# The weights' places cut into pieces, and the products of the projections' weights made in the head

## The chip, the core and the metric

The kernel runs on one NeuronCore of one Trainium2 chip. The metric is the time of one execution on the device in microseconds (us). The engines are named as in the profile: PE is TensorE (its matmuls; PEld its weight loads), DVE is VectorE, ACT is ScalarE, POOL is GpSimd, and SP is SyncE, which issues most of the transfers. All data are fp32.

## The reference

x holds 4 images of 128 channels and 64 x 64 pixels, so S = 4096 positions. Two layers follow one another, and the parts that the change touches are in the second one:

```
# layer 0
v = group_norm(x)
e1, e2 = prelu(w1 v), prelu(w2 v)                       # 64 channels each
asm = prelu(wa v)
x = x + softmax(e1^T e2, over the keys) applied to asm
# layer 1, tokens t = the positions of x, of 128 channels
n = layer_norm(t)
t = t + softmax((n Wq^T)(n Wk^T)^T / 128) (n Wv^T)
n = layer_norm(t)
p = softmax over the S tokens of (n gate + gate_b)      # 64 experts
vals, idx = top 8 tokens of each expert
pooled = sum over the 8 of vals * n[idx]                # one row for each expert and image
h = gelu([pooled, 1] weight1)                           # 128 -> 512, each expert its own
o = [h, 1] weight2                                      # 512 -> 128
t[idx] += vals * o
```

An expert's weight1 is 128 x 512 and its weight2 512 x 128, 256 KB each. All 64 experts are read once, 32 MiB, for only 4 rows each.

## The kernel before, in words

The kernel is one program with a fixed order on every engine. It goes through eight attention stages, `stage(b, layer, ...)`, in the order (image, layer) = (0,0), (1,0), (0,1), (2,0), (1,1), (3,0), (2,1), (3,1). A stage has 8 blocks n of 512 queries, and each block has 8 groups g of 512 keys. In a group PE makes the scores `ps` (L560), ACT their exponentials `pt` (L569), and PE the sums `av` (L494 for layer 0, L522 for layer 1, where DVE and PE also use combinations of tiles, `tt`, to save products). Work of other stages is given to a stage as a Python generator (`beside`, `ahead`); the stage takes one step of it in each group, so that PE makes it between two groups.

Ahead of the first stage lies the head. SP and ACT issue the 8 pieces of the first image, `first_x`; ACT then issues all the constants (`const_load`); `group_norm(0)` makes the statistics with DVE (`gn_st`), PE (`gn_pm`, `gn_pv`) and POOL (`gn_y`), and the first two blocks' convolutions (`pe`, `pa`, with their PReLU in `ye`, `te`, `ya`, `ta`) give the first operands.

`weights_qk()` makes the products of the projections' weights once: the transposes `pwq`, `pwk` (each copied to SBUF), their product `wqk`, and `wvd` with its sums `wtwo`, `wsum`. Before the change it is the last part of the generator beside the stage (0,0). The last row of weight1, a bias, is loaded as `w1b` and transposed by four PE transposes `pw` in stage (3,1), in `first_weights()`.

After the last stage comes the route of image 3 (`last_route`, `last_scores`), and then the expert products, in 16 groups g of 4 experts (EG). For each group `first_product` makes `ph` (copied to `hp`), `hidden` makes the transposes `pht`, adds the bias and applies the gelu (`hT`), and `second_product` makes `po`. A group's weights are 2 MiB, packed in DRAM by earlier transfers (`wp`), in two halves of 1 MiB: half 0 for `ph`, half 1 for `po`. They are loaded by SP into *places* in SBUF. A place before the change is one tile of 16 KB in each partition. There are nine:

- places 0 and 1 are the keys and values of the last stage, which come free late in it,
- 6, 7 and 2 are tiles of the pools `seq` and `extra`, loaded in stage (3,1),
- 3, 4 and 5 are a pool `ring`, opened when the pool `att` is closed after the last stage,
- 8 is `late_place`, in a pool `late`, opened when the pool `blk` is closed after the route.

A half is reloaded with group g + 9 when group g's product with it is made. A DMA on SP goes out in program order, and one that waits holds what stands behind it.

The softmax weights of image 3 are made on DVE, ACT and POOL in `last_scores`: a MATCH_REPLACE (L806) and two DVE steps that are spread between the groups, then exponentials on ACT (L985) and differences on POOL (L987). At the end, `first_pair` (the weights of images 0 and 1, 2 MiB) and `x2_pair` (the residual, 4 x 2 MiB) are loaded into places; PE makes `px` (L1276), DVE adds it to the residual (L1283), and ACT issues the stores (L1286).

`watch` and `keep_busy` are small extra instructions of PE and DVE that the kernel puts between parts of the program. They compute nothing that is returned.

Of the kernel before, what the change touches and what calls it, by code (L numbers as in the profile page):

```python
# [15 lines left out]
P = 128  # L16
BLK = 512
# [9 lines left out]
def tile_unshifted(  # L27
# [91 lines left out]

    def const_load(name, shape, src):  # L120
        t = const.tile(shape, F32, tag=name, name=name)
        nc.scalar.dma_start(out=t, in_=src)
        return t


# [9 lines left out]
    aa = const_load("aa_sb", [P, 1], a["aa"].partition_broadcast(P))  # L135
    wqT = const_load("wqT_sb", [P, P], a["WqT"])
    wkT = const_load("wkT_sb", [P, P], a["WkT"])
    wv = const_load("wv_sb", [P, P], a["WvT"])
    gate = const_load("gate", [P, E], a["gateT"])
    gate_b = const.tile([P, 1], F32, tag="gate_b", name="gate_b")  # L140
    w2b = const.tile([P, O], F32, tag="w2b", name="w2b")
    for h in range(2):
        half = slice(h * E, (h + 1) * E)
        nc.scalar.dma_start(out=gate_b[half, :], in_=a["gate_b"])
        nc.scalar.dma_start(out=w2b[half, :], in_=a["weight2"][:, H, :])

# [286 lines left out]
    def weights_qk():  # L433
        wT = []
        for nm, w in (("q", wqT), ("k", wkT)):
            pw = ms_tile(f"pw{nm}")
            nc.tensor.matmul(pw[:, :P], lhsT=w, rhs=unfold, start=True, stop=True)
            t = block_tile("te", f"w{nm}")[:, :P]
            nc.vector.tensor_copy(t, pw[:, :P])
            wT.append(t)  # L440
        yield
        pw = ms_tile("pwqk")
        nc.tensor.matmul(pw[:, :P], lhsT=wT[0], rhs=wT[1], start=True, stop=True)
        nc.vector.tensor_copy(wqk, pw[:, :P])
        yield
        pw = ms_tile("pwv")
        nc.tensor.matmul(pw[:, :P], lhsT=unfold, rhs=wv, start=True, stop=True)
        nc.vector.tensor_copy(wvd[:, :C], pw[:, :P])
        nc.vector.tensor_copy(wvd[:, C : C + 1], last[:, 0:1])
        lo, hi = slice(0, HC), slice(HC, C)  # L450
        for half in (lo, hi):
            nc.scalar.copy(wtwo[half, :], wvd[hi, :])
            nc.scalar.copy(wsum[half, :], wvd[lo, :])
        nc.vector.tensor_add(wsum, wsum, wtwo)
        yield
# [177 lines left out]
    def finish_attn(b, n):  # L633
# [28 lines left out]
        xq = resid.pop((b, 1, n)).rearrange("p (s c) -> p s c", c=C)  # L662
        xT = block_tile("inv", f"xT{nm}").rearrange("p (s c) -> p s c", c=C)
        for k, (s0, ns) in enumerate(((2, 2), (0, 2)) if final else ((0, 3), (3, 1))):
# [309 lines left out]
    def last_scores(b, top, neg):  # L974

        hs = half_of(b)
        m = M[b // 2][hs, :]
        z = late_place[hs, :]

        tc.keep_in_program_order(replace(b, top, z))  # L980
        yield
        for part in QUARTERS:
            for t in (z, m):
                tc.keep_in_program_order(
                    nc.scalar.activation(t[:, part], t[:, part], AF.Exp, bias=neg[hs, :])  # L985
                )
            nc.gpsimd.tensor_sub(m[:, part], m[:, part], z[:, part])  # L987
        yield
# [81 lines left out]

    packing = iter(())
    run(group_norm(0, first_x))
    first_conv = conv(0, first_x)
    for _ in range(2):
        next(first_conv)
    run(query(0, 0, 0))
    tc.no_sync_barrier()


    W, places_of = {}, {}  # L1080

    def place(i, t):
        if len(t.shape) == 3:
            t = t.rearrange("p j c -> p (j c)")
        places_of[i] = t.rearrange("p (h x) -> p h x", h=2)

    def new_place(i, pool, tag):
        place(i, pool.tile([P, 2 * EG * H], F32, tag=tag, name=f"w{i}"))

    def load(g, i, h):  # L1090
        W[g] = places_of[i]
        nc.sync.dma_start(out=W[g][:, h, :], in_=packed[g][:, h, :])

    w1bT = const.tile([P, NHC, E], F32, tag="w1bT", name="w1bT")

    def first_weights():

        watch(0)
        w1b = block_tile("xq", "w1b", 4)[:E, :]
        nc.sync.dma_start(out=w1b, in_=a["weight1"][:, D1 - 1, :])  # L1100
        yield from idle(2)
        new_place(6, seq, "k")
        new_place(2, extra, "w")
        for g in (6, 2):
            for h in range(2):
                load(g, g, h)
        yield from idle(2)
        pw = ms_tile("pw")
        for c in range(NHC):
            nc.tensor.transpose(  # L1110
                pw[:, bass.ts(c, E)], w1b.rearrange("e (p c) -> e c p", c=NHC)[:, c, :],
                ident[:E, :E],
            )
        nc.scalar.copy(w1bT.rearrange("p c e -> p (c e)"), pw[:, : NHC * E])
        yield from idle(2)
        new_place(7, seq, "v")
        for h in range(2):
            load(7, 7, h)
        yield

    def last_weights(n, g):

        if (n, g) == (0, 0):
            place(0, keys[B - 1, 1])
            place(1, values[B - 1, 1])
        if n == NB - 1:
            if g == NG // 2 - 1:
                load(0, 0, 0)
            if g == NG // 2:
                load(1, 1, 0)  # L1130
            if g == NG - 1:
                load(0, 0, 1)

    stage(0, 0, chain(group_norm(1), conv(1), weights_qk()), (1, 0), ahead=first_conv, pace=(4, 3))
    packing = pack_weights()
# [13 lines left out]

    ends["att"].close()  # L1150
    pooledT = seq.tile([P, E, PAD], F32, tag="mixed", name="pooledT", bufs=1)
    nc.gpsimd.memset(pooledT, 0.0)
    nc.gpsimd.tensor_copy(pooledT[:, :, 0 : B - 1], pooled[:, :, 0 : B - 1])
    while after:
        step_after()
    ring = ctx.enter_context(tc.tile_pool(name="ring", bufs=3, reuse_waits="tile"))
    load(1, 1, 1)
    for g in range(3, 6):
        new_place(g, ring, "w")
        for h in range(2):  # L1160
            load(g, g, h)
    keep_busy(FILL[4], "busy_d")
    last_top = last_route(B - 1, pooledT)
    ends["blk"].close()
    late = ctx.enter_context(tc.tile_pool(name="late", bufs=1, side="right", reuse_waits="tile"))
    late_place = late.tile([P, S], F32, tag="z", name="late_place")
    place(8, late_place)
    scores = last_scores(B - 1, *last_top)
    watch(1)

    for h in range(2):
        load(8, 8, h)
    outT = late.tile([P, B, E], F32, tag="outT", name="outT")
    osb = late.tile([P, E // EG, O], F32, tag="osb", name="osb")
    half_g = E // EG // 2
# [3 lines left out]
    def first_product(g):  # L1179
        ph = ms_tile(f"ph{g}")  # L1180
        for j in range(EG):
            nc.tensor.matmul(  # L1182
                ph[bass.ts(j, PAD), :], lhsT=pooledT[:, g * EG + j, :],
                rhs=W[g][:, 0, bass.ts(j, H)], start=True, stop=True,
            )
        hps[g] = hp = late.tile([P, H], F32, tag="hp", name=f"hp{g}", bufs=2)
        nc.vector.tensor_copy(hp, ph)

    def hidden(g):
        pt, hp = pht[:, g % 2, :], hps.pop(g)  # L1190
        for c in range(NHC):
            nc.tensor.transpose(  # L1192
                pt[:, bass.ts(c, P)], hp.rearrange("p (q c) -> p c q", c=NHC)[:, c, :], ident
            )
        hTs[g] = hT = late.tile([P, NHC, EG, PAD], F32, tag="hT", name=f"hT{g}", bufs=2)
        nc.vector.tensor_tensor(
# [5 lines left out]
    def second_product(g):  # L1202
        half, k = divmod(g, half_g)
        if k == 0:
            pos[half] = sc_tile(f"po{half}").rearrange("p k c -> p (k c)").rearrange(
                "p (g o) -> p g o", o=O
            )
        w2 = W[g][:, 1, :].rearrange("p (e c o) -> p e c o", e=EG, c=NHC)
        hT = hTs.pop(g)
        for c in range(NHC):  # L1210
            for j in range(EG):
                nc.tensor.matmul(  # L1212
                    pos[half][bass.ts(j, PAD), k, :], lhsT=hT[:, c, j, :], rhs=w2[:, j, c, :],
                    start=(c == 0), stop=(c == NHC - 1),
                )
        if k == half_g - 1:
            nc.vector.tensor_copy(osb[:, bass.ts(half, half_g), :], pos[half])
            for q in range(half * half_g // EG, (half + 1) * half_g // EG):
                by_expert(q)

    def by_expert(q):

        pt = ms_tile(f"pot{q}")
        for k in range(EG):
            nc.tensor.transpose(pt[:, bass.ts(k, P)], osb[:, q * EG + k, :], ident)
        nc.vector.tensor_copy(
# [4 lines left out]
    for g in range(E // EG + 2):  # L1231
# [6 lines left out]

        for half, now in ((0, g), (1, g - 2)):
            if 0 <= now and now + 9 < E // EG:  # L1240
                load(now + 9, now, half)
        if g == half_g + 2:
# [4 lines left out]

    M[0] = places_of[7].rearrange("p h x -> p (h x)")
    tc.keep_in_program_order(nc.sync.dma_start(out=M[0], in_=first_pair))
    WIDE = 2 * BLK  # L1250
    HS = S // 2
    ys = []
    for i in range(B // 2):
        for q in range(2):
            ys.append(places_of[2 * i + q])
            tc.keep_in_program_order(
# [7 lines left out]
    for i in range(B // 2):  # L1264
# [7 lines left out]
        for n in range(NB):  # L1272
            px = sc_tile(f"px{i}_{n}")
            for h in range(2):
                hs = slice(h * E, (h + 1) * E)
                nc.tensor.matmul(  # L1276
                    px[:, h, :], lhsT=oe[hs, :], rhs=M[i][hs, bass.ts(n, BLK)],
                    start=True, stop=True,
# [552 lines left out]
```

## Time and profile before

| | us |
|---|---|
| median of 3 runs (lowest to highest) | 3269.55 (3269.16 to 3271.02) |
| the profiled execution | 3268.95 |
| its span | 3267.2 |
| busy: PE | 3227.5 (99% of the span) |
| busy: DVE | 2123.3 (65%) |
| busy: ACT | 1255.6 (38%) |
| busy: POOL | 425.4 (13%) |
| DMA, mean over the span | 68 GB/s |
| DMA, last of 40 equal slices | 398 GB/s |

The span runs from the first instruction to the last one of the profiled execution; its time also holds what lies around them. Busy shares are means over the whole span. The head and the end are short against it, so the means say nothing of them: they are read from the chain of waits (what released each piece of work, followed back from the end), the timeline, and tables by stretches of time.

### The profile page before, as it was taken

Reading aid. Unit: us, or ns where it says so; the run is one execution under the profiler, and the core shown is the slowest. Engines: PE = TensorE matmul, PEld = TensorE weight load, DVE = VectorE, ACT = ScalarE, POOL = GpSimd, SP = SyncE. Lnnn points to the kernel's source line nnn. Section 1 sums busy time; section 2 is a strip of 40 time slices with the busy share of each in tenths; the row PEclk is TensorE's granted clock in tenths of the full one; section 3 lists DMA queues with packets and bytes.
Section 4 is the critical chain, followed back from the end, with each engine's and each line's share of the span. In section 5 each row is a group of like instructions: output and inputs, shape, how many; then the busy total and the mean of one; then the engine's idle time right before and its main releaser. Section 6 shows DMA issues by size and latency. Waiting matters only on the chain.

```text
span 3267.2 us, 49620 instructions
## 1 busy us (share of the span) xinstructions
PE 3227.5 (99%) x19856; PEld 1544.2 (47%) x19856; DVE 2123.3 (65%) x4191; ACT 1255.6 (38%) x1437; POOL 425.4 (13%) x414
## 2 busy tenths in 40 slices
PE   8999999999999999999999999999999999999997
PEld 4444444444554544444554444444445444445453
DVE  6665567556676667755675657775676566676566
ACT  3333434333333345333333335333333333343332
POOL 0111112310000004141000002242100002010011
PEclk9999999999999999999999999999999999999998
DMA  3121244223333222311221111321131111131149
GB/s 84 52 55 27 58 112 120 76 78 89 84 80 86 58 53 53 68 36 30 49 43 30 38 29 39 88 68 26 40 71 37 33 28 32 23 105 43 27 184 398
DMA packets 364242, 222.93 MB, mean 68 GB/s; under 512 B 273504, under 2 KB 298336, under 8 KB 358624
## 3 DMA queue, kind: packets, MB, share of 16 engines
q1 hardware_dynamic: 358544, 208.15, 23.8%
q10 hardware_dynamic: 4944, 10.46, 0.8%
q8 instruction: 158, 2.59, 0.3%
q0 software_dynamic: 512, 1.05, 0.1%
q14 instruction: 84, 0.69, 0.1%
HBM read 159.75 MB, written 97.19 MB: 79 GB/s over the span
## 4 chain that ended last, share of the span: by engine, by line
PE 97%; DVE 1%; DMA 1%; issue 0%; POOL 0%; ACT 0%; SPq 0%; ACTq 0%; DVEq 0%; POOLq 0%
PE ps L560 41%; PE av L494 27%; PE av L522 24%; PE pe L273 1%; PE pq L463 1%; PE pv L681 1%; PE pa L301 1%; DMA tt<-x 1%; PE pg L748 0%; PE ph L1182 0%; PE pd L608 0%; PE po L1212 0%; PE pht L1192 0%; PE px L1276 0%; DMA first_x<-in_x_dram 0%
## 5 line engine op out<-in xcount | busy, mean ns | idle before, releaser
L569 ACT ACTIVATE pt<-ps 128x1024 f32<-128x1024 f32 x1024 | 1022.2, 1025 | 1514.6 <-PE ps L560 1432.3
L560 PE MATMUL ps<-q,t 128*64 128x512 f32 x4096 | 924.8, 592 | 0.0
L494 PE MATMUL av<-pt,asm 64*128 64x512 f32 x4096 | 922.7, 589 | 0.9 <-ACT sw L652 0.9
L584 DVE TENSOR_TENSOR sacc<-sacc,pt 128x1024 f32<-128x1024 f32 x448 | 586.4, 1309 | 288.1 <-ACT pt L569 262.7
L522 PE MATMUL av<-pt,tt 128*64 128x256 f32 x3072 | 636.2, 379 | 0.0
L494 PEld LDWEIGHTS av<-pt,asm 64*128 64x128 f32 x4096 | 397.0, 187 | 484.5 <-issue 468.4
L508 DVE TENSOR_TENSOR tt<-pt 128x512 f32<-128x512 f32 x512 | 354.2, 692 | 356.3 <-ACT pt L569 339.8
L522 PE MATMUL av<-tt,mixed 128*64 128x256 f32 x2048 | 525.6, 379 | 0.0
L560 PEld LDWEIGHTS ps<-q,t 128*64 128x64 f32 x4096 | 292.2, 137 | 489.2 <-issue 458.1
L522 PEld LDWEIGHTS av<-pt,tt 128*64 128x64 f32 x3072 | 353.9, 137 | 290.8 <-issue 143.4
L560 PE MATMUL ps<-e,e 64*128 64x512 f32 x2048 | 490.0, 596 | 0.5 <-ACT ye L275 0.5
L522 PE MATMUL av<-tt,tt 128*64 128x256 f32 x1024 | 304.7, 379 | 0.0
L522 PE MATMUL av<-pt,mixed 128*64 128x256 f32 x1024 | 304.6, 379 | 0.0
L560 PEld LDWEIGHTS ps<-e,e 64*128 64x128 f32 x2048 | 192.6, 187 | 228.1 <-issue 223.1
L522 PEld LDWEIGHTS av<-tt,mixed 128*64 128x64 f32 x2048 | 280.5, 137 | 2.7 <-DVE tt L508 0.2
L182 POOL TENSOR_TENSOR l_y<-l_v,mhalf 128x4 f32<-128x4 f32 x64 | 64.8, 1013 | 1612.6 <-DVE l_v L181 1612.3
L510 DVE TENSOR_TENSOR tt<-pt 128x256 f32<-128x256 f32 x512 | 220.4, 431 | 16.4
L509 DVE TENSOR_TENSOR pt<-tt,pt 128x256 f32<-128x256 f32 x512 | 219.7, 429 | 16.2
L522 PEld LDWEIGHTS av<-pt,mixed 128*64 128x64 f32 x1024 | 140.2, 137 | 72.9 <-DVE pt L509 0.3
L522 PEld LDWEIGHTS av<-tt,tt 128*64 128x64 f32 x1024 | 140.1, 137 | 1.5 <-DVE tt L510 0.3
L603 POOL TENSOR_TENSOR all_sum<-all_sum,c 128x512 f32<-128x512 f32 x32 | 44.0, 1376 | 515.4 <-DVE c L602 515.4
L183 DVE TENSOR_TENSOR l_z<-l_y 128x4 f32<-128x4 f32 x64 | 13.9, 217 | 91.5 <-POOL l_y L182 91.5
(267 smaller groups left out, 1795.0 us busy)
## 6 DMA issues: line engine op xcount, KB each, us to landing
wp<-in_weight_dram SPq DMA_DIRECT2D x128, 256.0 KB, 4.9
w<-wp SPq DMA_DIRECT2D x22, 1024.0 KB, 11.4
xq<-in_x_dram SPq DMA_DIRECT2D x32, 256.0 KB, 3.8
rb<-inv SPq DMA_DIRECT2D x32, 256.0 KB, 3.4
xT<-xt SPq DMA_DIRECT2D x128, 64.0 KB, 2.2
ak<-xT SPq DMA_DIRECT2D x32, 256.0 KB, 3.1
t<-kt SPq DMA_DIRECT2D x128, 64.0 KB, 2.2
t<-t SPq DMA_DIRECT2D x32, 256.0 KB, 3.2
```

Source lines behind the costliest of these rows:

```text
L182: nc.gpsimd.tensor_tensor(y[:, :k], v[:, :k], mhalf[:, :k], op=ALU.pow)
L273: nc.tensor.matmul(pe[part, :], lhsT=w12[:, part], rhs=xn, start=True, stop=True)
L301: nc.tensor.matmul(pa[part, bass.ts(s, P)], lhsT=xn[:, bass.ts(s, P)][:, part], rhs=wa, start=True, stop=True,)
L494: nc.tensor.matmul(avs[b, 0, n][:, r, :], lhsT=values[b, 0][rows, j, :], rhs=pt[rows, h, :], start=(j == 0), stop=(j == NJ - 1),)
L508: nc.vector.tensor_sub(tt[:, 0:2, :], p4[:, :, 1, :], p4[:, 0, :, :])
L509: nc.vector.tensor_add(p4[:, 0, 1, :], tt[:, 1, :], p4[:, 0, 0, :])
L510: nc.vector.tensor_sub(tt[:, 2, :], p4[:, 1, 0, :], p4[:, 0, 1, :])
L522: nc.tensor.matmul(av[bass.ts(half, HC), bank, slot, :], lhsT=lhsT, rhs=rhs, start=first, stop=final, skip_group_check=True,)
L560: nc.tensor.matmul(ps[part, h, :], lhsT=key[:, part], rhs=q[rows, :], start=True, stop=True,)
L569: nc.scalar.activation(pt, ps, AF.Exp, scale=scale)
L584: nc.vector.tensor_add(sums[b, n], sums[b, n], pt)
L603: nc.gpsimd.tensor_add(all_sum, all_sum, c1)
```

## The change

It has three parts.

1. **Constants.** wqT, wkT, wv, gate, the two parts of gate_b and of w2b (8 transfers) are issued by SP rather than ACT, and w1b is loaded by SP in the head.
2. **Products.** `weights_qk()` is run in the head: its first step (pwq, pwk) ahead of `group_norm(0)`, its others after it. The four transposes pw of w1b follow in the head. The copies out of PSUM go from DVE to ACT; those of wtwo and wsum and an addition go to POOL.
3. **Places.** A place may now be made of pieces: `piece(i, h, t, g)` adds a tile t to half h of place i, and loads its part of group g's weights into it. The tiles are those of the attention's own pools (`q`, `xq`, `inv`, `pt`, `sx`, `sw`, `tb`, `xp`, and the rest of `mixed`), taken over in the order in which they come free; the pools `ring` and `late` are gone. There are nine places and a half: half 0 is reloaded with group g + 10, half 1 with g + 9. The tiles `hp`, `hT`, `osb` and `outT` are taken from existing tags too, and the last images' `xT` is made in place of `xq`. `last_scores` works in place 7, and `first_pair` is loaded as 8 pieces of 256 KB into the pieces of place 8 (before, one transfer of 2 MiB into place 7).

The diff, cut to its core:

```diff
+    wqT = const_load("wqT_sb", [P, P], a["WqT"], nc.sync)
+    wkT = const_load("wkT_sb", [P, P], a["WkT"], nc.sync)
+    wv = const_load("wv_sb", [P, P], a["WvT"], nc.sync)
...
-    gate = const_load("gate", [P, E], a["gateT"])
+    gate = const_load("gate", [P, E], a["gateT"], nc.sync)
...
-            nc.vector.tensor_copy(t, pw[:, :P])
+            nc.scalar.copy(t, pw[:, :P])
...
-        nc.vector.tensor_copy(wqk, pw[:, :P])
+        nc.scalar.copy(wqk, pw[:, :P])
...
-        nc.vector.tensor_copy(wvd[:, :C], pw[:, :P])
+        nc.scalar.copy(wvd[:, :C], pw[:, :P])
...
-            nc.scalar.copy(wtwo[half, :], wvd[hi, :])
+            nc.gpsimd.tensor_copy(wtwo[half, :], wvd[hi, :])
...
-        xT = block_tile("inv", f"xT{nm}").rearrange("p (s c) -> p s c", c=C)
+        xT = xq if final else block_tile("inv", f"xT{nm}").rearrange("p (s c) -> p s c", c=C)
...
-        z = late_place[hs, :]
+        z = z_place[hs, :]
...
+    w1b = block_tile("xq", "w1b", 4)[:E, :]
+    nc.sync.dma_start(out=w1b, in_=a["weight1"][:, D1 - 1, :])
+    projections = weights_qk()
+    next(projections)
     run(group_norm(0, first_x))
+    run(projections)
     first_conv = conv(0, first_x)
-    for _ in range(2):
-        next(first_conv)
+    next(first_conv)
+    next(first_conv)
+    pw = ms_tile("pw")
+    for c in range(NHC):
+        nc.tensor.transpose(...)
+    nc.scalar.copy(w1bT.rearrange("p c e -> p (c e)"), pw[:, : NHC * E])
...
+    def piece(i, h, t, g):
+        t = t.rearrange("p k c -> p (k c)") if len(t.shape) == 3 else t
+        got = pieces.setdefault((i, h), [])
+        j = sum(k for _, k, _ in got)
+        got.append((j, t.shape[1] // H, t))
+        load_piece(g, h, got[-1])
+
+    def load_piece(g, h, p):
+        j, k, t = p
+        nc.sync.dma_start(out=t, in_=packed[g][:, h, j * H : (j + k) * H])
...
                 load(0, 0, 0)
+                piece(8, 0, block_tile("q", "w8_2"), 8)
+                piece(8, 0, block_tile("xq", "w8_3", 4), 8)
             if g == NG // 2:
                 load(1, 1, 0)
+                piece(8, 1, block_tile("xq", "w8_4", 4), 8)
+            if g == NG // 2 + 1:
+                piece(8, 1, block_tile("xq", "w8_5", 4), 8)
+                piece(8, 1, block_tile("inv", "w8_6"), 8)
+                piece(8, 1, block_tile("inv", "w8_7"), 8)
             if g == NG - 1:
+                for i in range(2):
+                    piece(4, 0, att_tile("pt", 6, f"w4_{i}"), 4)
                 load(0, 0, 1)
...
-    stage(0, 0, chain(group_norm(1), conv(1), weights_qk()), (1, 0), ahead=first_conv, pace=(4, 3))
+    stage(0, 0, chain(group_norm(1), conv(1)), (1, 0), ahead=first_conv, pace=(4, 3))
...
-    ends["att"].close()
...
+    for i in range(2):
+        piece(4, 1, att_tile("pt", 6, f"w4_{2 + i}"), 4)
+    for i in range(2):
+        piece(5, 0, att_tile("sx", 4, f"w5_{i}"), 5)
+    load(1, 1, 1)
+    for i in range(2):
+        piece(5, 1, att_tile("pt", 6, f"w5_{2 + i}"), 5)
+    for i in range(2):
+        piece(6, 0, att_tile("sx", 4, f"w6_{i}"), 6)
+    piece(6, 1, block_tile("q", "w6_2"), 6)
...
-    ring = ctx.enter_context(tc.tile_pool(name="ring", bufs=3, reuse_waits="tile"))
-    load(1, 1, 1)
-    for g in range(3, 6):
-        new_place(g, ring, "w")
-        for h in range(2):
-            load(g, g, h)
+    piece(6, 1, block_tile("sw", "w6_3", 1), 6)
+    piece(6, 1, block_tile("xq", "w6_4", 4), 6)
...
-    ends["blk"].close()
-    late = ctx.enter_context(tc.tile_pool(name="late", bufs=1, side="right", reuse_waits="tile"))
-    late_place = late.tile([P, S], F32, tag="z", name="late_place")
-    place(8, late_place)
+    piece(9, 0, mixed_place[:, E * PAD :], 9)
+    piece(6, 1, block_tile("tb", "w6_5"), 6)
+    for i in range(2):
+        piece(9, 0, block_tile("xp", f"w9_{i}"), 9)
+    z_place = whole[7]
...
-        hps[g] = hp = late.tile([P, H], F32, tag="hp", name=f"hp{g}", bufs=2)
+        hps[g] = hp = block_tile("c0", f"hp{g}")
...
-            nc.vector.tensor_copy(osb[:, bass.ts(half, half_g), :], pos[half])
-            for q in range(half * half_g // EG, (half + 1) * half_g // EG):
-                by_expert(q)
+            for i in range(half_g // EG):
+                q = half * half_g // EG + i
+                osb = block_tile("u", f"osb{q}").rearrange("p (k o) -> p k o", o=O)
+                nc.vector.tensor_copy(osb, pos[half][:, bass.ts(i, EG), :])
+                by_expert(q, osb)
...
-        for half, now in ((0, g), (1, g - 2)):
-            if 0 <= now and now + 9 < E // EG:
-                load(now + 9, now, half)
+        for half, now, ahead in ((0, g, 10), (1, g - 2, 9)):
+            if 0 <= now and now + ahead < E // EG:
+                load(now + ahead, now, half)
...
-    M[0] = places_of[7].rearrange("p h x -> p (h x)")
-    tc.keep_in_program_order(nc.sync.dma_start(out=M[0], in_=first_pair))
+    for n in range(NB):
+        tc.keep_in_program_order(
+            nc.sync.dma_start(out=first_M[n], in_=first_pair[:, bass.ts(n, BLK)])
+        )
```

## The prediction

> **What bounds the kernel now.** I read the engine rows and the chain of the page first, to see which engine sets the time; then the chain of waits at the places that the change touches.
>
> ```profile
> PE 3227.5 (99%) x19856; PEld 1544.2 (47%) x19856; DVE 2123.3 (65%) x4191; ACT 1255.6 (38%) x1437; POOL 425.4 (13%) x414
> PE 97%; DVE 1%; DMA 1%; issue 0%; POOL 0%; ACT 0%; SPq 0%; ACTq 0%; DVEq 0%; POOLq 0%
> ```
>
> PE is busy for 99% of the span and makes 97% of the chain. So nothing on another engine pays between about 26 us (PE's first long run) and 3157 us (its last), and whatever is taken out of PE's order there pays in full. The two ends are the only places where something else decides. The head, from the chain:
>
> ```profile
> 2.21 6.50 DMA first_x<-in_x_dram
> ...
> 8.73 1.30 DVE gn_st L208 x2
> ...
> 10.05 0.38 DVE gn_mv L211
> ...
> 10.57 0.57 PE gn_pm L214 x2
> ...
> 25.85 2.09 PE ps L560 x7
> ```
>
> The last piece of the first image lands at 8.71; the statistics reach PE at 10.57; PE runs without a gap from 25.85. PE is free between these, but DVE and ACT are on the chain. The projections' products in the stage (0,0), from the chain:
>
> ```profile
> 271.76 0.40 PE pd L608 x8
> ...
> 272.18 0.97 DVE inv L613
> ...
> 273.19 0.49 PE pwk L437 x2
> 273.68 1.92 PE ps L560 x8
> ...
> 279.03 0.42 PE pwqk L443 x2
> ...
> 284.80 0.42 PE pwv L447 x2
> ...
> 2944.25 0.62 PE pw L1110 x4
> ```
>
> PE stands still for about 1 us there, waiting for DVE to empty a small PSUM buffer, and then makes the products. Last the end, by stretches (start:end, length, busy time of PE, PEld, DVE, ACT, POOL, then clock, DMA share, GB/s):
>
> ```profile
> 3152.00:3156.00 4.00, 4.00 (x42) 2.63 (x40) 1.94 (x4) 0.47 (x1) 0.00 (x0) 1.00 0.75 262
> 3156.00:3158.00 2.00, 2.00 (x19) 1.33 (x16) 0.00 (x0) 0.48 (x1) 0.50 (x1) 1.00 0.00 0
> 3162.00:3260.00 98.00, 81.62 (x886) 45.13 (x886) 63.64 (x109) 24.74 (x35) 10.35 (x5) 0.92 1.01 419
> ```
>
> and by the timeline (in brackets the idle time of the engine before it, and what ended it):
>
> ```profile
> 3206.45 4.42 DVE L806 MATCH_REPLACE8 late_place<-r_top,M 64x4096 f32<-64x4096 f32 x1
> ...
> 3211.09 1.94 PE L1182 MATMUL ph<-w,pooledT 128*32 128x512 f32 x8 [1.98 <-DVE count L1775]
> ...
> 3217.74 0.75 PE L1192 MATMUL pht<-ident,hp 128*128 128x128 f32 x4 [0.81 <-DVE hp L1187]
> ...
> 3236.17 2.34 DVE L1283 TENSOR_TENSOR t<-t,px 128x1024 f32<-128x1024 f32 x2
> ```
>
> The DMA engines are full from 3160 to 3262, yet moved nothing in 3156–3158, while loads stood behind the closing of a pool. Beside that stream runs a chain that is nearly as long: expert products, a stall of PE behind one 4.42 us DVE instruction, slower groups after it, the 16 additions.
>
> The profiled execution has a span of 3267.2 and a time of 3268.95, 1.75 around it; it is 0.6 below the median, 3269.55. I sum against it and add the 0.6 back.
>
> **The change part by part.**
>
> *Products out of the stages.* pwq and pwk: from 271.76 to the next ps at 273.68 the chain loses 1.92, of which pd's 0.40 was due anyway, less 0.04 of gaps: 1.56 − 0.04 ≈ 1.5. pwqk and pwv: 0.42 each, and the ps group after each takes 1.92 where an undisturbed one takes 1.72: 0.62 each. The four transposes pw: 0.62, and the ps group after them 3.58 instead of 3.43: 0.77. Sum 1.5 + 1.24 + 0.77 ≈ **−3.5 us**, on PE's own path with nothing to take its place. The copies that go to ACT and POOL were off the path; wtwo and wsum are not read until the keys of stage (1,0), hundreds of us later: 0.
>
> *The head.* Eight constant loads leave ACT's queue for SP's. In the old trace ACT issues them from 9.83 to 14.14, then loads its table for 1.28 and idles to ye at 16.78. In the new order ACT holds 4 pieces of x, 7 constants, the table load and the copies wq, wk, wqk, wvd before ye. PE gets pwq and pwk ahead of gn_pm, and gn_pm takes a PSUM buffer of a rotation of two, so it waits until ACT has copied wq. With half of the image's pieces on each queue, the seventh load of the set now waits for the last piece of x (8.71); after it come three constants (0.4–0.9 each as at 8.03–9.74), so ACT is done issuing at about 11.0; table to 12.3, copy (0.35 for 128x128, an estimate from the 0.62 of a 64x512 copy at 18.74) to 12.65. gn_pm then starts at 12.7, not 10.57: **+2.1**. PE queues gn_pm, gn_pv and pe behind it, and all of the chain to 25.85 follows. pwqk and pwv slip between gn_pv and pe, where PE waits for DVE anyway; pw (0.62) stands before the second pe, which waits for DVE: 0.1. Bounds: +0.5, if ACT's issues end at 9.5, since then only the table load stands in the way; +3.2, if the copies also hold up ye. DVE's new order (te before asm in the second block) gives at most 0.7 back. I take **+2.2**. The loads on SP land before 15 (w1b issued at about 12.5, 2–3 us), and pw needs it at 17.6; SP's own next issue on the chain is e<-ye at 23.52, long after. POOL gets four small copies and an add behind wvd, at about 16 us; its one step on the chain, gn_y, is before them, and only the last column's copy, which waits for nothing, before that. Both 0; should the loads take 2 us longer than that, PE's queue stands as long (rival E).
>
> *Places of pieces.* Half a place more (reloads fall from 14 halves to 13), and the loads of groups 8, 4 and 5 are issued before 3157. In the stretches 3128–3158 DMA has room. From the order on SP I count 2 MiB (group 8), 1 (4, first half) and about 1.2 moved before 3158. After 3151.44 40 MiB remain, by 419 GB/s 100 us: 3253.5 if there were no gap. But SP takes its queue in order, and one load waits for the pool product that ends at 3175.7: the 9 MiB issued ahead of it are done by about 3175.5, and with the landing of the first next load 2.9 us go idle: DMA alone would end at 3256.5 rather than 3263.1: −6.6.
>
> The chain beside it gains less. MATCH_REPLACE now stands before hp of group 10 on DVE: 3204.7 to 3209.1, hp to 3209.9. PE then still has ph11 and pht10 to make and idles about 3.3 us, where it idled 1.98. Afterwards ph stays one group ahead of pht in the new order, so that the groups keep 2.55 us, as from 3184 to 3204, instead of the 3.43 that the wait at 3217.74 shows. From 3209.9: 3.1 (ph, pht at the slow clock) + 4 × 2.55 + 1.7 (po, pht) + 1.4 (bias, gelu) = 3226.3 for the last gelu; it was 3227.86. First addition 8.3 later, as before, 3234.6; sixteen in 21.0: 3255.7; the last stores, 1 MiB behind a short queue, 2.5 + 2 for issue and landing: 3260.1, against 3263.1: **−3.0**. Bounds −1 (the slow clock lasts, or the additions wait for x2) and −6.6 (DMA alone).
>
> Two rules speak against this part. First the clock: after 1.98 idle the granted clock was 0.75 in 3210–3212 and 0.50 in 3212–3214, and ph, pht, po took 1.94, 1.12, 1.24 where 1.07, 0.75, 1.08 is usual: 1.4 us lost. The Trainium skill (TensorE: Matmul & The Clock Gate, Part 1: The HAM clock gate) has half clock after an idle window of about 3.4 us and full clock after as long a busy one; by it the longer stall costs 3.4/2 = 1.7. I keep the row: 0.3 apart. Second, small pieces: the eight 256 KB pieces of x ran at 380 to 405 GB/s together (4–8 us), the 1–2 MiB loads at 419. The skill's SBUF — State Buffer, The DMA setup-cost knee, gives 224 GB/s for one 256 KiB transfer and says to coalesce; the 11 MiB that are now in pieces of 256 and 512 KB would by that take up to 24 us more, by the row under 2. Up to eight are in flight, so the row decides.
>
> Sum: −3.5 + 2.2 − 3.0 = −4.3; 3268.95 − 4.3 = 3264.65, with the 0.6 back 3265.25, told as **3265.2**.
>
> **The rivals.**
>
> *B, the queue alone sets the end.* PE's stall is not longer, the additions follow the stream: −6.6 at the end. 3269.55 − 3.5 + 2.2 − 6.6 = 3261.6; with the head at +0.5, 3259.9. For: 101% DMA share in 98 us. Against: additions take 21.0 us after a chain that gains 1.6.
>
> *C, the gains are small at both ends.* Head +3.2, end −1: 3268.2. For: the table load stands before the copy that PE waits for. Against: the wait needs all ACT's issues late.
>
> *D, slower: SP starves the stream.* SP issues in order; a piece that waits for its tile (the pool product at 3175.7) holds all weights behind it. Each us of empty DMA is a us of the end. With 9 MiB ahead the hole is 2.9; if pieces run at the skill's 224 GB/s, or the first pieces wait for the last attention group as before, loads come later than the groups need them. The early loads are worth 6.6 + 2.9 = 9.5, the middle less the head 1.3: slower than before from about 11 us of hole, by 0.2% from 17.5; a hole of 20 gives 3278. Against: the fast rows of small pieces.
>
> *E, the change does not do what it says* (the products' loads come so late that PE waits in the head for them, +2 more): 3267, inside C.
>
> **How the numbers follow.** 0.2% is 6.5 us, 3263.0 to 3276.1, about what a measurement of this kernel can tell from no change. My case has 0.50 (own range 3263 to 3267), B 0.33, C with E 0.12, D 0.05. Faster by over 0.2%: B's 0.33 and 0.09 of mine, 0.42; slower 0.04, most of D; the same 0.54. The range runs from B's low end, 3259.5, to C's, 3268.5; what is left out is D, and edges of B and C, under 0.2.
>
> **What would show it.** Head: gn_pm at about 12.7 behind ACT's copy of wq, the first unbroken ps at 28. Middle: no pwk, pwqk, pwv, pw; stage (1,0) begins 2.7 us earlier relative to the first ps. End: DMA share near 0.9 from 3152, a hole near 3176, MATCH_REPLACE before hp of group 10, groups at 2.55 after it, last gelu 1.5 earlier relative to the end of the attention, additions back to back. I am wrong if gn_pm keeps its 10.6, if the additions wait for x2, or if DMA idles for more than 4 us after the attention.

## The result, and the profile after

The changed kernel takes 3263.81 us (median of 20 runs, 3262.92 to 3266.58) against 3269.89 for the kernel before (20 runs, 3268.89 to 3271.02). The ratio is 0.9982 with a 95% interval of 0.9976 to 0.9989: faster by 5.9 us, between 3.6 and 7.9 (the medians differ by 6.1). The forecast was 3265.2, in a range of 3259.5 to 3268.5.

The profiled execution of the changed kernel took 3263.81 with a span of 3262.0; that of before 3268.95 with 3267.2. The 5.2 us between the spans are what the traces can account for. PE's place in them is read at the same piece of work in both, from the chain of waits (start, length, what):

| PE reaches | before | after | after − before |
|---|---|---|---|
| gn_pm, the image's statistics | 10.57 | 13.10 | +2.53 |
| the second group's ps, from which PE never stops | 25.85 | 28.70 | +2.85 |
| the ps group behind pwv's place | 285.22 | 285.45 | +0.03, since before's group there still takes 0.20 longer (1.92 against 1.72) |
| last av | 3151.40 | 3150.57 | −0.83 |
| end of the span | 3267.2 | 3262.0 | −5.2 |

The head, in the chain of the changed kernel:

```profile
11.44 1.28 ACT L441
12.73 0.28 ACT wq L441
...
13.10 0.57 PE gn_pm L216 x2
...
19.38 0.70 ACT ye L277
...
20.12 2.08 PE pa L303 x8
22.20 1.71 PE pe L275 x2
24.84 1.92 PE ps L562 x8
...
28.70 2.08 PE ps L562 x7
```

L441 is ACT's table load and the copy of wq. PE's gn_pm starts right after that copy, not when the statistics are ready. Further down stands a second wait: pa starts after ACT's ye, which it did not before.

The stage (0,0), where the products were; pd is followed at once by ps:

```profile
274.59 0.35 PE pd L610 x8
274.95 1.92 PE ps L562 x8
276.87 3.43 PE av L496 x16
```

And the end, by stretches (start:end, length, busy time of PE, PEld, DVE, ACT, POOL, then clock, DMA share, GB/s) and by the timeline:

```profile
3152.00:3156.00 4.00, 4.00 (x40) 2.65 (x38) 1.22 (x3) 0.00 (x0) 0.00 (x0) 1.00 0.94 360
3156.00:3158.00 2.00, 2.00 (x18) 1.56 (x14) 0.69 (x1) 0.59 (x1) 1.33 (x1) 1.00 1.03 420
...
3174.00:3176.00 2.00, 1.60 (x17) 1.21 (x20) 0.84 (x6) 1.04 (x1) 0.00 (x0) 1.00 0.77 285
3176.00:3178.00 2.00, 2.00 (x20) 0.82 (x12) 1.72 (x7) 0.00 (x0) 0.00 (x0) 1.00 0.62 168
3178.00:3180.00 2.00, 2.00 (x13) 0.47 (x11) 1.56 (x3) 0.63 (x1) 0.00 (x0) 1.00 0.82 307
```

```profile
3202.68 4.42 DVE L808 MATCH_REPLACE8 w<-r_top,M 64x4096 f32<-64x4096 f32 x1
...
3207.88 1.38 PE L1227 MATMUL ph<-tt,mixed_place 128*32 128x512 f32 x8 [3.12 <-DVE count L1829]
```

The two microseconds 3156–3158, empty before, are full now. In their place a hole stands at 3174–3180, where the DMA engines moved 253 GB/s on average instead of the 422 of before: 6 us × 169 GB/s = 1.0 MB, 2.4 us of transfers. PE stands still for 3.12 us at MATCH_REPLACE where it stood for 1.98.

### The profile page after: what moved, and what is told of

Read it like the earlier page. It is cut to its first block, busy times and chain, and to the rows that moved or that the text cites. A ratio compares the mean times of both kernels' runs of the same rounds, so it can differ in the third digit from the quotient of the medians.

```text
span 3262.0 us, 49665 instructions
## 1 busy us (share of the span) xinstructions
PE 3226.9 (99%) x19856; PEld 1571.9 (48%) x19856; DVE 2118.8 (65%) x4187; ACT 1255.1 (38%) x1437; POOL 431.1 (13%) x420
## 4 chain that ended last, share of the span: by engine, by line
PE 98%; DVE 1%; issue 0%; DMA 0%; ACT 0%; ACTq 0%; POOL 0%; DVEq 0%; POOLq 0%
PE ps L562 41%; PE av L496 27%; PE av L524 24%; PE pe L275 1%; PE pa L303 1%; PE pq L465 1%; PE pv L683 1%; PE ph L1227 1%; PE pg L750 0%; PE po L1259 0%; PE px L1330 0%; PE pd L610 0%; PE pht L1237 0%; DMA first_x<-in_x_dram 0%; DVE w L1337 0%
## 5 line engine op out<-in xcount | busy, mean ns | idle before, releaser
L562 PE MATMUL ps<-q,t 128*64 128x512 f32 x4096 | 934.6, 592 | 0.0
L562 PEld LDWEIGHTS ps<-q,t 128*64 128x64 f32 x4096 | 304.7, 137 | 482.3 <-issue 452.6
```

The lines of the kernel that those rows point to most:

```text
L562: nc.tensor.matmul(ps[part, h, :], lhsT=key[:, part], rhs=q[rows, :], start=True, stop=True,)
```

## The experiments

Two questions were open. What made the head dearer than reckoned? And what ends the program now: the chain of expert products and additions, as the prediction had it, or the stream of transfers? All ratios are against the kernel before, with their 95% intervals; the last column is the median less the change's 3263.81.

| kernel | median, us | ratio | to the change |
|---|---|---|---|
| the change | 3263.81 | 0.9982 (0.9976–0.9989) | |
| head_only | 3267.93 | 0.9995 (0.9987–1.0003) | +4.1 |
| places_only | 3266.19 | 0.9991 (0.9984–0.9997) | +2.4 |
| head_late | 3262.46 | 0.9979 (0.9971–0.9987) | −1.4 |
| after_warm | 3263.44 | 0.9982 (0.9974–0.9990) | −0.4 |
| nine | 3266.33 | 0.9989 (0.9980–0.9997) | +2.5 |
| no_match | 3263.94 | 0.9984 (0.9978–0.9991) | +0.1 |
| no_pair | 3263.81 | 0.9984 (0.9977–0.9990) | 0.0 |
| neither | 3259.68 | 0.9971 (0.9958–0.9983) | −4.1 |
| small | 3268.42 | 0.9998 (0.9989–1.0006) | +4.6 |
| best2 | 3261.45 | 0.9975 (0.9966–0.9985) | −2.4 |
| best3 | 3262.03 | 0.9976 (0.9967–0.9985) | −1.8 |
| best4 | 3261.78 | 0.9976 (0.9966–0.9985) | −2.0 |

The intervals are some 2 to 4 us wide on either side, so differences of 1 us between two of these kernels are read from their traces and not from the medians. The kernel before, measured beside each of them again, had medians of 3269.55 to 3269.89. Executions of one kernel with the places of pieces differ by 2 to 5 us, and their traces are of two kinds, with full or half clock in the first group products (last section); so a trace is compared with one of the same kind where that matters.

**The two halves of the change: head_only and places_only.** The kernel before with constants and products moved, and the changed kernel with constants and products where they were.

> Constants and products as in the change, places as before. If the three parts simply add, as the offsets between the two traces say (PE 2.85 us later when its unbroken run begins, 2.81 won back in stage (0,0), 0.76 in stage (3,1)), this kernel is 0.7 us faster than before: 3269.2. If the head's delay is a matter of the places as well (w1b's tile), it is equal to before or slower. By the prediction's terms (2.2 and 3.5) it would be 1.3 faster: 3268.6.

> The places of pieces alone; constants and products as before. The tail's gain between the traces is 5.2 - 0.8 = 4.4 us: 3265.5 if that stands by itself. By the prediction's term it would be 3.0: 3266.9. If the two parts lean on each other, the two single kernels do not sum to the 6.1 us of the change.

Medians: 3267.93 and 3266.19, 1.6 and 3.4 us below before's 3269.55; the sum, 5.0, is not distinguishable from the change's 6.1. In head_only's trace the last av starts at 3150.53 (−0.87 against before) and the span is 1.1 shorter; the median is 0.7 below the lower of the two expected, which stays unexplained, and as a time it is not beyond the noise. In places_only's trace the last av starts at 3151.38, as before. So by the medians about two thirds of what the change brings comes from the places (3.4 of 5.0). The trace of places_only shows only 2.0 between the spans where 4.4 were expected: its execution took 3267.39, 1.2 above its median, and PE ran its first groups at half clock there (last section), which is the likely reason.

**The head: head_late and after_warm.** The first makes pwq and pwk after the group norm's products:

```diff
-    next(projections)
     run(group_norm(0, first_x))
     run(projections)
```

> The changed kernel with pwq and pwk made after group_norm's products instead of ahead of them. Theory: the head's delay is PE standing behind gn_pm, which waits for ACT's copy of wq, itself behind ACT's issues and table load. Then gn_pm is back at about 10.6 to 11.1 (the image lands 0.5 later), the unbroken run starts 2 to 2.5 us earlier, and the time is 3261.3 to 3261.8. Rival: the delay is the image's pieces sharing the DMA with eight more early constants, or PE's extra products before the second block; then at most 0.5 comes back, 3263.3 or more.

The timeline of PE in head_late (start, length; in brackets the idle time before):

```profile
10.53 0.56 PE L216 MATMUL gn_pm<-gn_mv,avg_g 128*128 128x1 f32 x2 [10.53 <-DVE gn_mv L213]
...
12.23 0.77 PE L439 MATMUL pwq<-unfold,wqT_sb 128*128 128x128 f32 x2
...
16.95 0.74 PE L1086 MATMUL pw<-ident,w1b 64*128 64x64 f32 x4
17.79 2.08 PE L303 MATMUL pa<-wa_sb,xk 128*128 128x128 f32 x8
19.66 1.91 PE L275 MATMUL pe<-xk,w 128*128 128x512 f32 x2
```

gn_pm is back at 10.53, as before the change (10.57), and it waits for the statistics (gn_mv). The last av starts at 3148.25, 2.32 earlier than in the change, and the span is 2.2 shorter. The theory's 2 to 2.5 is met; eight more early constants cost the image nothing that shows. The time expected is met by the profiled execution, 3261.49, and not by the median, which fell by 1.4 only. What remains of the head, 0.7 us, is pw: between pe and pa it takes one of two PSUM buffers, so that pa (17.79) waits for the other one until ye is made. Before, pa started at 16.54, right behind pe.

after_warm leaves the order of the change and has ACT load its table early:

```diff
+    warm = const.tile([1, 1], F32, tag="warm", name="warm")
+    nc.vector.memset(warm, 0.0)
+    nc.scalar.activation(warm, warm, AF.Exp)
     def const_load(name, shape, src, queue=None):
```

> The changed kernel with a 1x1 exponential on ACT behind its four image loads, so that ACT's table is loaded at about 3 us and not at 11.4. ACT's issues still end at 11.4, so the copy of wq starts at 11.45 instead of 12.73, gn_pm at 11.8 instead of 13.1, and the program ends 1.3 us earlier: 3262.5. If gn_pm waits for something else than that copy: 3263.8. If the table load delays ACT's later issues by its 1.28: 3263.8 too, but with ACT's issues ending at 12.7.

The table is loaded at 2.71, the copy of wq starts at 11.70 instead of 12.73, gn_pm at 12.06 instead of 13.10, and the last av at 3149.17, 1.40 earlier. So that copy is what gn_pm waits for. The end followed by 0.8 in the trace and 0.4 in the median (3263.44, where 3262.5 was expected), less than PE's 1.4: the rest was lost again behind the last stage. In the trace the pool product still comes 1.39 earlier (3172.40) and the transfers end 1.1 earlier (3257.2 against 3258.4), so only a small part of it is lost before that.

**What ends the program: nine, no_match, no_pair, neither.** nine takes the half place away again:

```diff
-        for half, now, ahead in ((0, g, 10), (1, g - 2, 9)):
+        for half, now, ahead in ((0, g, 9), (1, g - 2, 9)):
...
-    piece(9, 0, mixed_place[:, E * PAD :], 9)
...
-    for i in range(2):
-        piece(9, 0, block_tile("xp", f"w9_{i}"), 9)
```

> The changed kernel without the half place more: half 0 of group 9 is loaded into place 0 when group 0 is made, as before. Same bytes in all, 1 MiB later. Theory that the DMA queue sets the end: the queue runs dry 2.4 us earlier while PE waits for the route, and the end is 2.4 later: 3266.2. Theory of the prediction, that the chain of products and additions sets it: 0 to 0.5, 3263.8 to 3264.3.

Measured 3266.33, 2.5 above the change. By stretches:

```profile
3174.00:3176.00 2.00, 1.60 (x14) 1.25 (x18) 0.76 (x5) 1.12 (x1) 0.00 (x0) 0.94 0.06 20
3176.00:3178.00 2.00, 2.00 (x12) 0.54 (x8) 1.11 (x7) 0.00 (x0) 0.00 (x0) 0.50 0.00 0
3178.00:3180.00 2.00, 2.00 (x16) 0.71 (x12) 0.98 (x3) 0.00 (x0) 0.00 (x0) 0.71 0.81 213
```

The hole is 78 GB/s over 6 us where the full stream gives 422, 2.1 MB or 4.9 us, against 2.4 us in the change, and the median moved by that difference. That the two agree so well is chance in part: this execution ran its first groups at half clock (0.50 above), the change's did not, and their spans differ by 3.4 (3265.4 and 3262.0). Beside no_pair below, whose trace has half clock there too, nine moved 252 GB/s instead of 330 in 3168–3184: 1.2 MB, 3.0 us. Its fastest and its slowest execution are both 1.5 above the change's. So the half place is worth 1.5 to 3 us, and what it does is fill the wait for the route; the 0 to 0.5 of the prediction's theory is refuted.

The next three leave out the one, the other and both:

```diff
-        tc.keep_in_program_order(replace(b, top, z))
...
-    for n in range(NB):
-        tc.keep_in_program_order(
-            nc.sync.dma_start(out=first_M[n], in_=first_pair[:, bass.ts(n, BLK)])
-        )
```

> The changed kernel without the 4.42 us MATCH_REPLACE (left out: the marking of the chosen tokens of image 3, so its weights are wrong). PE's stall of 3.1 to 3.4 us goes, the clock does not fall, and the products and additions finish about 3.5 to 5 us sooner. Prediction's theory, the chain of products and additions ends the program: 3258.8 to 3260.3. Queue theory, the stream of transfers ends it and the chain only has to keep ahead of it: at most the backlog that stands after the last addition in the changed kernel counts against it, so 3262.8 to 3263.8, and the transfers end 7 us or more after the last addition instead of 5.

> The changed kernel without the load of first_pair, 2 MiB in 8 pieces (left out: the weights of images 0 and 1 in the last products, which take what lies in those tiles). 2 MiB take 5.0 to 5.3 us of the queue. Queue theory: the end comes earlier until the chain's own tail stops it; the last addition ends at 3253.3 and a lone store needs some 2.5, so about 2.5 to 3 of the 5 show: 3261. Chain theory: 3263.5 to 3264, nothing.

> Both omissions at once: without MATCH_REPLACE and without the load of first_pair (so the weights of all images in the last products are wrong). Each alone moved nothing. Theory of a tie: in the changed kernel the chain of products and additions and the stream of transfers end at the same time, so that taking one away leaves the other. Then both together give the smaller of the two gains, about 5 us: 3258.8 to 3260. Rival: something third ends the program, such as the pace of the additions with their stores, whatever stands ahead of it: then again nothing, 3263 to 3264.

no_match: 3263.94, nothing, as the queue theory had it. no_pair: 3263.81, nothing, as the chain theory had it. Each refutes one of the two. neither: 3259.68, 4.1 below, and the slowest of its six executions, 3261.21, is faster than the change's fastest, 3262.92. The chain of waits of no_match shows an addition that waits 9.37 us for a store to land:

```profile
3233.93 9.37 DMA out_dram<-t
...
3243.32 1.22 DVE w L1336
```

and the stretches of no_pair show a queue that is no longer full when the additions begin:

```profile
3230.00:3235.00 5.00, 2.04 (x9) 0.69 (x8) 5.00 (x5) 5.00 (x6) 5.00 (x3) 1.00 0.69 287
3235.00:3240.00 5.00, 4.18 (x16) 1.20 (x16) 4.80 (x5) 0.70 (x1) 4.06 (x2) 1.00 0.50 197
```

The last eight additions, with the stretch in which the transfers end, in the change, no_match, no_pair and neither:

```profile
3243.47 9.79 DVE L1337 TENSOR_TENSOR w<-w,px 128x1024 f32<-128x1024 f32 x8
...
3258.00:3260.00 2.00, 0.00 (x0) 0.00 (x0) 0.00 (x0) 0.00 (x0) 0.00 (x0) 0.50 0.18 68
```

```profile
3238.36 9.88 DVE L1336 TENSOR_TENSOR w<-w,px 128x1024 f32<-128x1024 f32 x8
...
3256.00:3258.00 2.00, 0.00 (x0) 0.00 (x0) 0.00 (x0) 0.00 (x0) 0.00 (x0) 0.50 0.85 332
3258.00:3260.00 2.00, 0.00 (x0) 0.00 (x0) 0.00 (x0) 0.00 (x0) 0.00 (x0) 0.50 0.12 41
```

```profile
3244.18 9.79 DVE L1333 TENSOR_TENSOR w<-w,px 128x1024 f32<-128x1024 f32 x8
...
3258.00:3260.00 2.00, 0.00 (x0) 0.00 (x0) 0.00 (x0) 0.00 (x0) 0.00 (x0) 0.50 0.35 129
```

```profile
3238.99 9.79 DVE L1332 TENSOR_TENSOR w<-w,px 128x1024 f32<-128x1024 f32 x8
...
3252.00:3254.00 2.00, 0.00 (x0) 0.00 (x0) 0.00 (x0) 0.00 (x0) 0.00 (x0) 0.57 0.61 244
```

Put side by side (the end of the transfers is worked out from the shares of the last stretches):

| | last addition ends | transfers end | between |
|---|---|---|---|
| before | 3257.2 | 3263.1 | 5.9 |
| the change | 3253.3 | 3258.4 | 5.1 |
| no_match | 3248.2 | 3258.0 | 9.8 |
| no_pair | 3254.0 | 3258.7 | 4.7 |
| neither | 3248.8 | 3253.2 | 4.4 |

What the chain needs by itself is read from no_pair, whose queue is not full when the additions begin: its transfers end 4.7 behind the last addition. Even there the stores alone fill the queue from 3240 on: an addition puts out 512 KB each 1.22 us, 430 GB/s, and the queue moved 405 in 3240–3250. So what counts of the chain is when its additions begin. neither has 4.4, but its queue is full to the end (403 GB/s in 3240–3250), so it does not show the chain alone. The change has 5.1: chain and stream end within about half a us of each other. It is a tie, so that taking away either alone leaves the other, and both together bring the 4 to 5 us. One reserve: in no_pair's trace PE ran its first groups at half clock, and its additions begin 1.6 later than the change's (3234.36 and 3232.80), so this trace alone does not give the chain's end; the three times together do, and no_pair's fastest execution, 3262.89, gained nothing on the change's 3262.92 either.

**The size of a transfer: small.** Each load of weights that goes through `load` is cut into transfers of 256 KB (11 pieces of 512 KB, loaded for the first time by `piece`, stay whole):

```diff
-        for p in pieces[i, h]:
-            load_piece(g, h, p)
+        for j, k, t in pieces[i, h]:
+            for m in range(k):
+                load_piece(g, h, (j + m, 1, t[:, m * H : (m + 1) * H]))
```

> The changed kernel with every load of weights cut into transfers of 256 KB (23 MiB of loads of 512 KB and 1 MiB are cut; same bytes, same places). The trace of the change shows 397 to 401 GB/s in stretches with pieces where whole loads ran at 416 to 430. If the size of a transfer is what costs that, about 5% of 20 MiB, 2.5 us: 3266.3. If the skill's 224 GB/s for one such transfer applied, over 20 us: above 3280. If eight in flight make up for it, 3263.8.

Measured 3268.42: 4.6 lost, so none of the three numbers was met; it lies between the first and the skill's. The stretch 3182–3220, full in all three kernels: before, the change, small.

```profile
3182.00:3220.00 38.00, 34.65 (x541) 20.89 (x540) 22.77 (x31) 7.56 (x12) 0.00 (x0) 0.96 1.02 421
```

```profile
3182.00:3220.00 38.00, 34.88 (x554) 21.11 (x548) 22.47 (x31) 7.41 (x13) 0.00 (x0) 0.96 1.02 406
```

```profile
3182.00:3220.00 38.00, 34.88 (x547) 20.91 (x536) 22.04 (x31) 7.55 (x12) 0.00 (x0) 0.96 1.04 377
```

All three are 100% busy by the share of time, and move 421, 406 and 377 GB/s. The share does not show what a small transfer costs; the GB/s column does. The 29 GB/s over 38 us are 2.7 us, most of the 3.1 between the spans of the change and small (3262.0 and 3265.1); small's profiled execution is its fastest, 3266.85.

**Better versions: best2, best3, best4.** best2 is head_late with pw made behind the last stage (w1b in a tile that is free by then) and the early table; best3 puts pw behind the route's transposes l; best4 adds PE fillers in two gaps behind the route.

```diff
+    w1b = block_tile("u", "w1b")[:E, :]
...
     keep_busy(FILL[0], "busy_a")
+    pw = ms_tile("pw")                           # best2
+    ...
+    pw = sc_tile("pw")[:, 0, :]                  # best3, best4
+    ...
     keep_busy(FILL[4], "busy_d")
```

> Three edits on the changed kernel: pwq and pwk after group_norm's products (as in head_late); the transposes pw moved out of the head, to behind the last stage, where PE has fillers (w1b is loaded in stage (3,1) into a free tile); and a 1x1 exponential on ACT behind its four image loads, so that the table is loaded there. In head_late pw's place in the rotation of two PSUM buffers makes pa wait for ye: the second pe starts at 19.66 where it was 18.24 before. If that is all that is left, PE starts its unbroken run at 26.2 instead of 27.2, and the time is 3262.5 - 1.0 = 3261.5. If pw behind the last stage holds up the route, up to 0.7 of it is lost: 3262.2.

> As best2, but with the transposes pw behind the transposes l of the last route and in a PSUM tile of the scores' pool, instead of ahead of pv in the small rotation. In best2 the route from the end of the attention to the pool product took 0.73 us longer than in head_late (23.95 against 23.22 from the last av's start). If that was pw's place in the rotation, 0.5 to 0.7 comes back: 3260.8. If pw costs the route its own time wherever it stands: 3261.5.

> best3 with four 128x128 filler products on PE in each of two gaps behind the last route (0.46 us between the transposes pzT and the pool product, 0.41 us between it and the first ph). Theory: the profiled executions fall into two kinds by the clock that PE has when the group products start (first two groups 1.92 us at clock 1.00, 3.2 to 3.6 us at 0.5 to 0.7), and PE's idle gaps there let the clock fall. Then with the fillers the first two groups take 1.92, the late half of the times goes, and the median falls to 3261.0 to 3261.4 from best3's 3262.0. If the short gaps are not what lets the clock fall, 3262.0 with the same spread.

best2: 3261.45, as expected in number, though not step by step: the second ps started at 25.79, as early as before the change (25.85), and the last av 0.83 earlier than in head_late; but pw ahead of pv held the route up by 0.73, so that the pool product came only 0.1 earlier, and the span is 0.4 shorter. best3 got 0.66 of it back (the pool product 23.29 behind the start of the last av, best2 23.95), and then PE made its first two groups in 3.33 instead of 1.92; 3262.03. best4's first two groups took 1.92, but each filler of 128x128 took about 0.29, and the first ph came 1.4 later than in best3, 0.5 of which stood already at the last av; 3261.78, with the same spread (3260.75 to 3263.21). The times give its theory no support; what the clocks say of it is in the last section. The three are not distinguishable from one another; they are the fastest complete kernels here, and against the change their intervals overlap.

## Why the prediction was right, point by point

**Products out of the stages, −3.5.** PE made up 2.85 − 0.03 = 2.82 in the stage (0,0), reckoned 2.74, and the last av's −0.83 leaves 0.86 for pw in the stage (3,1), reckoned 0.77. (1.92 less 0.40 is 1.52 and not 1.56; the 1.5 stands.) Right in mechanism and size; nothing took their place.

**The head, +2.2: right in its mechanism, too small.** It is 2.85. gn_pm came at 13.10 and not 12.7, because ACT's issues ended at 11.40 and not 11.0; the order (issues, table, copy, gn_pm) is as worked out, and head_late and after_warm each show a link of it. The other part is the term for pw, set at 0.1 because it "stands before the second pe, which waits for DVE": in truth pw sits in a rotation of two PSUM buffers, and pa ahead of it had to wait for ye. head_late still has 0.7 of that.

**The end, −3.0: right in sign, and the step that failed is which of the two ends it.** The span shows −4.4 behind the last stage. The prediction set the chain 3.6 us later than the stream and let the chain decide alone. Both terms were off, in opposite directions:

- The stream was reckoned to end at 3256.5 on the old time axis. The sum holds 2.0 us that it does not name: 3151.44 and 100 us make 3251.5 and not 3253.5, so its own terms give 3254.4. no_match, where the stream alone decides, has 3258.0, or 3258.9 with the 0.83 of the head and stages put back, 4.5 later. By the change's rows 4.1 of that are: 42.5 MB left at 3151.4 and not 41.9 (1.3 us), 357 GB/s from there to 3158 (1.0), 406 in 3160–3174 (0.4), 409 instead of 419 in 3180–3258 (1.9), and, the other way, a hole of 2.4 and not 2.9. The price of pieces, "under 2", was about right as a size and was not put into the sum.
- The chain was reckoned to end at 3260.1, and has about 3258.8 with the same 0.83 put back (3253.3 + 4.7 + 0.8). MATCH_REPLACE came at 3202.7, where 3204.7 less the shift is 3203.9: this execution made its first two groups in 1.92, while the sum took over the 3.22 of the old trace. So the last gelu, at 3224.45 instead of 3227.86, came 2.6 earlier relative to the attention's end, not 1.5. The rest went as worked out: a stall of 3.12 (reckoned 3.3), slow clock after it (0.63 and 0.52), the groups then at 2.55, additions in 20.5 (reckoned 21.0).

In bytes the stream's account closes: 43.5 MB were left to move after 3158 before the change, 40.1 after it. These 3.4 MB are 8.1 us at 421 GB/s; the hole takes 2.4 back, the lower rate in 3180–3258 1.9 and that in 3160–3174 (406 against 418) 0.4; the start of the stream at 3158–3160, slow before (164 GB/s), gives 1.2: 4.6, and the transfers end 4.7 earlier.

**The rivals.** B had the right bound and the wrong price: the stream does end the program as much as the chain does, at −4.4 and not −6.6. C did not occur. D did not either: the hole was 2.4, far from the 11 from which it decides; but nine shows its mechanism at work: a longer hole, a later end. E did not occur: PE waited for wqT until 9.55, a microsecond ahead of the statistics.

**The range and chances.** The time lies in the likeliest case's own range (3263 to 3267). The interval of the ratio, −3.6 to −7.9 us, lies on both sides of the 6.5 that was set as the bound of "faster". That the sum came so near is luck in part: the head was set too small by 0.65 and the gain at the end too small by 1.4, with opposite effects on the time, and the end's number was taken from the chain alone, while the stream ends with it.

## What to carry to other kernels

When a stage is bounded by two things that lie close together, price both to the end and take the later one; then removing either shows nothing, and only removing both tells. Count a full queue by the bytes it moves, not by its busy share: pieces let loads start earlier, and cost rate (421 to 406 to 377 GB/s here). Before work is moved into an idle gap, follow its PSUM buffer: with a rotation of two, a copy that is late by one engine's queue holds the next product on another.

## What the runs showed of the hardware that was not expected

- Whether PE has full clock when the group products start differs from execution to execution. The line of the first groups in the chain of places_only, and the one in the change:

```profile
3176.33 3.50 PE ph L1222 x16
```

```profile
3175.53 1.92 PE ph L1227 x16
```

  The granted clock in 3174–3180 was 0.72 in the one and 1.00 in the other, with the same instructions and the same idle time of 0.40 ahead. In the kernel before, the queue is full then (1.01 in 3174–3180), so PE's delay there need not reach the stream; in the changed one the hole ends with PE's first release, so it does: places_only's hole is 225 GB/s against 253. That would account for the wider spread of the changed kernel's times (3262.9 to 3266.6, before 3268.9 to 3271.0). The mean clock of each execution, known to three digits, agrees: the change's 12 executions with 0.998 or more took 3262.92 to 3264.24, the 8 with 0.997 took 3263.80 to 3266.58. But the mean does not tell where the clock was lost, so this is inferred, and what decides between the two kinds stays open. With best4's fillers 7 of 10 executions had 0.998, in best3 2 of 12; the times did not narrow.
- The Trainium skill (TensorE: Matmul & The Clock Gate, Part 1: The HAM clock gate) has the clock fall after an idle window of about 3.4 us that runs free of the program. The stall of 1.98 us gave 0.75 and 0.50 in the old trace, that of 3.12 gave 0.63 and 0.52: less idle time than a window is enough, and the longer stall did not cost more.
- The 224 GB/s that the skill gives for one 256 KiB transfer (SBUF — State Buffer, The DMA setup-cost knee) do not bind a stream with several in flight: small moved 377 GB/s in a stretch of little but such loads, each of which took 5.6 us from issue to landing, so that some eight were in flight (5.6 us at 377 GB/s are 2.1 MB). But the 380 to 405 of the image's load were not the whole price either: small lost 4.6 us.
